# A second matmul layer as seven block products for eight, on pairs of token tiles, in a kernel of twelve expert passes

## The chip, the cores and the metric

The kernel runs as one program on one core of a Trainium2 chip. The metric is the device time of one execution in microseconds, the median of several; smaller is better.

## The reference, cut to what matters

Everything is float32. There are two samples of 2048 tokens with 512 channels. Two shared experts and one expert chosen per sample are each a two-layer network with a hidden width of 2048; a softmax gate per sample mixes their three outputs, and a second layer, with a 512 x 512 matrix chosen per sample, follows. Both layers have a residual.

```
dense(x, wi, wo) = relu(x @ wi) @ wo
s0, s1 = dense(x, swi[0], swo[0]), dense(x, swi[1], swo[1])
eo     = dense(x, wi[label[b]], wo[label[b]])
w      = softmax(relu(concat(eo[:, 0], s0[:, 0], s1[:, 0]) @ g1) @ g2)
x      = x + eo * w[0] + s0 * w[1] + s1 * w[2]      # the mix
out    = x + x @ W[cat[b]] + bias[cat[b]]            # the second layer
```

## The kernel before, in words

**Blocks and units.** The 4096 tokens are four blocks of 1024. The work is a list of twelve units (n = 0 to 11): the two shared experts on the four blocks (n = 0 to 7), then the chosen experts, two blocks of sample 0 (n = 8, 9) and two of sample 1 (n = 10, 11). A unit is `up` (L762, the first matrix) and `down` (L903, the second). Both already use a seven-product scheme in two levels, so each is 49 products; the sums around them are on VectorE and GpSimd.

**Slots.** The order of all engines is written out by hand. `up` goes through 7 x 14 = 98 slots, each with two matmuls of 128x256; `down` goes through 49 slots (`SLOTS_DN`, L433), each with four. Within every slot, after its matmuls, `step(other_bg)` (L658) takes one step of the *first* generator in the list `other_bg`, up to its next `yield`; only when that one has ended does the next in the list begin. So side work gets one step per slot, 147 steps per unit, in the order in which it was appended.

**Side work at the end.** After unit 8 the gate of sample 0 (`gate`, L1096) and the second layer of its first block (`layer1`, L1185) are appended; after unit 9 the second layer of the next block; at the start of unit 10 the part of sample 1's gate that belongs to the shared experts (`gate_shared`, L1070); after unit 10 sample 1's `gate` and `layer1` of the third block; at the first slot of `down` in unit 11 `premix` (L1228) for the fourth block. At the last slot but one of `down` in unit 11, `prepare` (L1321) empties the list: `while other_bg: step(other_bg)` (L1333). Then `last_layer1` (L1270) does the second layer of the fourth block with nothing beside it.

**`layer1`.** `layer1_weights` (L1144) loads the 1 MB matrix into the buffer tagged "s" (there is one), waits 14 slots, adds the identity to its diagonal (the residual), and makes the bias by a matmul. Then for each of eight tiles of 128 tokens: `fetch` loads four parts of 256 KB (the input and three expert outputs) into one of three buffers, tagged "raw", "o" and "t"; `mix` scales three of them on ScalarE (L1205) and adds them on GpSimd (L1210); `layer1_mm` (L1170) runs four matmuls of 128x512 into one PSUM tile; `layer1_put` (L1178) adds the bias on VectorE and stores. `mix` of a tile is issued a whole tile ahead of its matmuls. One tile takes 7 slots.

**`premix`** loads two 1 MB accumulators, three 1 MB pieces of earlier outputs into the buffers "raw", "o" and "t", then the matrix of the fourth block into "s"; it makes 16 multiply-adds on VectorE (L1251), and a fourth piece is loaded after the first four of them.

All loads and stores named here are issued by SyncE's queue (SP), in order; an instruction there that waits holds up those behind it.

Of the kernel before, what the change touches and what calls it, by code (L numbers as in the profile page):

```python
# [8 lines left out]
F32 = mybir.dt.float32  # L9
AF = mybir.ActivationFunctionType  # L10
# [5 lines left out]
P = 128  # L16
TB = 1024
TQ = 256
NP = 7
ADD, SUB = ALU.add, ALU.subtract  # L20
# [16 lines left out]
def cond_resid_kernel(  # L37
# [22 lines left out]
    nc = tc.nc  # L60
    B, S, D = x.shape
    E, _, F = wi.shape
    NCAT = W.shape[0]
    NX = g2.shape[1]
    DC = D // P
    NG = F // P // 4
    NBB = S // TB
# [10 lines left out]
    bigp = ctx.enter_context(tc.tile_pool(name="big", bufs=1))  # L78
    iop = ctx.enter_context(tc.tile_pool(name="io", bufs=2))
    small = ctx.enter_context(tc.tile_pool(name="small", bufs=1))  # L80
    ps = ctx.enter_context(tc.tile_pool(name="ps", bufs=2, space=PSUM))
# [4 lines left out]
    def read_ids():  # L86
# [22 lines left out]
    units = [(e, blk) for e in range(2) for blk in range(NB)]  # L109
# [12 lines left out]
    xr = {blk: dram.tile([P, 16, TQ], F32, name=f"xr_{blk}") for blk in range(NB)}  # L122

    xs = {blk: dram.tile([P, NP, NP, TQ], F32, name=f"xs_{blk}") for blk in range(NB)}
    ys = {
        (j, blk): dram.tile([P, DC, TB], F32, name=f"ys_{j}_{blk}")
        for j in range(NX)
        for blk in range(NB)
    }
# [526 lines left out]
    prep_bg, other_bg = [], []  # L656
# [400 lines left out]
    gates, hids = {}, {}  # L1057
# [5 lines left out]
    def when(there):  # L1063
        while not there[0]:
            yield

    def when_quiet():
        yield from when(quiet)
# [73 lines left out]
    NT = TB // P  # L1142

    def layer1_weights(blk, lag, also=None):  # L1144

        b = blk // NBB
        brow = small.tile([1, D], F32, tag="brow", name=f"brow_{blk}")
        nc.sync.dma_start(out=brow, in_=bvec[bass.ds(cat[b], 1), :])
        w1 = bigp.tile([P, DC, D], F32, tag="s", bufs=1, name=f"w1_{blk}")
        nc.sync.dma_start(out=w1, in_=W_v[:, bass.ds(cat[b] * DC, DC), :])  # L1150
        bias = small.tile([P, D], F32, tag="bias", name=f"bias_{blk}")
        for k in range(lag):
            yield
            if k == 5 and also:
                also()
        for c in range(DC):
            yield from when_quiet()
            v = w1[:, c, c * P : (c + 1) * P]
            nc.vector.tensor_tensor(v, v, ident, ADD)
            if c % 2:  # L1160
                yield
        pb = ps.tile([P, D], F32, tag="m", name=f"pb_{blk}")
        nc.tensor.matmul(pb, lhsT=ones[0:1, :], rhs=brow, start=True, stop=True)
        nc.vector.tensor_copy(bias, pb)
        l1[blk] = (w1, bias)
        yield

    l1, po = {}, {}

    def layer1_mm(blk, t, mixed):  # L1170
        po[t] = ps.tile([P, D], F32, tag="m", name=f"po_{blk}_{t}")
        for c in range(DC):
            nc.tensor.matmul(  # L1173
                po[t], lhsT=mixed[c], rhs=l1[blk][0][:, c, :],
                start=(c == 0), stop=(c == DC - 1),
            )

    def layer1_put(blk, t):  # L1178
        b, t0 = divmod(blk, NBB)
        o = iop.tile([P, D], F32, tag="xn", name=f"o_{blk}_{t}")  # L1180
        nc.vector.tensor_tensor(o, po[t], l1[blk][1], ADD)
        r0 = t0 * TB + t * P
        nc.sync.dma_start(out=out[b, r0 : r0 + P, :], in_=o)

    def layer1(blk, lag):  # L1185
        b = blk // NBB
        mixed = {}
        xv = xr[blk].rearrange("p (c q) t -> p c q t", c=DC)

        def fetch(t):  # L1190
            m = bigp.tile(
                [P, 4, DC, P], F32, tag=("raw", "o", "t")[t % 3], bufs=1, name=f"mix_{blk}_{t}"
            )
            q, h = divmod(t, 2)
            nc.sync.dma_start(out=m[:, 3, :, :], in_=xv[:, :, q, h * P : (h + 1) * P])
            for j in range(NX):
                nc.sync.dma_start(
                    out=m[:, j, :, :], in_=ys[j, blk][:, :, t * P : (t + 1) * P]
                )
            mixed[t] = m  # L1200

        def mix(t):
            m = mixed[t]
            for j in range(NX):
                nc.scalar.activation(  # L1205
                    m[:, j, :, :], m[:, j, :, :], AF.Copy, scale=gates[b][:, j : j + 1]
                )
            yield
            for j in range(NX):
                nc.gpsimd.tensor_tensor(m[:, 3, :, :], m[:, 3, :, :], m[:, j, :, :], ADD)  # L1210
                yield

        yield from layer1_weights(blk, lag, lambda: (fetch(0), fetch(1)))
        yield from mix(0)
        for t in range(NT):
            if t + 2 < NT:
                fetch(t + 2)
            if t + 1 < NT:
                yield from mix(t + 1)
            layer1_mm(blk, t, [mixed[t][:, 3, c, :] for c in range(DC)])  # L1220
            yield
            yield
            layer1_put(blk, t)
            yield

    acc = {}

# [63 lines left out]
    with tc.manual_schedule():  # L1291


        zero = small.tile([1, 512], F32, tag="brow", name="zero")
        nc.vector.memset(zero, 0.0)
        for k in range(2):
            pz = ps.tile([P, 512], F32, tag="z", name=f"prime_{k}")
            nc.tensor.matmul(pz, lhsT=ones[0:1, :], rhs=zero, start=True, stop=True)
        y = yp.tile([P, DC, 4, TQ], F32, tag="y", name="y_0")
        x_rest = first_x()  # L1300
        next(x_rest)
        begin = First(y)
        read_ids()
        xg = x_sums(0)
        advance(xg)
        fetch_w(7)
        begin.outer((5,))
        other_bg.append(("x0", x_rest))
        for n, (e, blk) in enumerate(units):
            if n == 0:  # L1310
                for e0, k0 in [(e0, k0) for e0 in range(1, NE) for k0 in range(2)]:
                    preps[e0, k0] = Prep(e0, k0)
            tops = {}
            if n in (2 * NB, 2 * NB + NBB):
                other_bg.append((f"s{n}", gate_shared((n - 2 * NB) // NBB, 13 if n == 2 * NB else 6)))
            if n:
                y = yp.tile([P, DC, 4, TQ], F32, tag="y", name=f"y_{n}")
            H = up(n, xg, tops, y)
            coming = {}

            def prepare(s, n=n, y=y):  # L1321
                m = n + 1
                if n == 0 and s == 30:

                    preps[1, 0].begin()
                elif n == 0 and s == len(SLOTS_DN) - 1:
                    begin.flush()
                    prep_bg.extend(preps.values())
                if m == len(units):
                    if s == 0:  # L1330
                        other_bg.append(("pre", premix(units[n][1], 10)))
                    elif s == len(SLOTS_DN) - 2:
                        while other_bg:  # L1333
                            step(other_bg)
                        for t in LAST[:2]:
                            last_mix(units[n][1], y, t)
                    return
                if m in MAKES:
                    if s == 0:
                        coming["x"] = load_x(m, 2)  # L1340
                    if s % 2 == 0:
                        next(coming.get("x", iter(())), None)
                    if s == 44:
                        for _ in coming.get("x", ()):
                            pass
                        coming["s"] = x_sums(m)
                    if s >= 44 and "r" not in coming and advance(coming["s"], 1):
                        coming["r"] = True
                elif s in (30, 38):
                    fetch_parts(m, I_UP(m)[(s - 30) // 8])  # L1350

            down(n, H, tops, y, prepare)
            if n + 1 < len(units):
                xg = coming.get("s")
                if xg and "r" not in coming:
                    advance(xg)
            if e >= 2:
                b = e - 2
                while prep_bg:
                    for part in "ost":  # L1360
                        prep_bg[0].force(part)
                    prep_bg.pop(0)
                if blk % NBB == 0:
                    other_bg.append((f"g{b}", gate(b, 8)))
                if n + 1 < len(units):
                    other_bg.append((f"l{blk}", layer1(blk, 14)))
        while other_bg:
            step(other_bg)
        last_layer1(blk, y)
# [30 lines left out]
```

## Time and profile before

| | us |
|---|---|
| median of 3 runs (2220.66 to 2226.8) | 2224.69 |
| the profiled execution | 2226.44 |
| its span | 2224.7 |
| TensorE matmuls busy | 2187.0 (98%) |
| VectorE busy | 1620.0 (73%) |
| GpSimd busy | 812.9 (37%) |
| ScalarE busy | 545.1 (25%) |

The granted TensorE clock is 0.997 of full. On the page, a busy share of an engine is its own time, and a group's line gives the busy sum, the mean of one, and the idle time of the engine ahead of the group with what ended it. The chain of waits is the one that ended last, followed back. A float32 matmul stands in the trace as two weight-load and matmul pairs, so four matmuls are "x8"; the time between starts, and not the duration of one, is its cost, since they overlap.

### The profile page before, as it was taken

To read this page: it belongs to the slowest core of one execution; us is meant where nothing else is said; L and a number is where in the kernel's file an instruction comes from. 1 tells how busy PE (TensorE), PEld (TensorE's weight loads), DVE (VectorE), ACT (ScalarE), POOL (GpSimd) and SP (SyncE) were. 2 spreads that over 40 slices of the span, in tenths; PEclk is the share of its full clock that TensorE was granted. 3 is DMA by queue.
4 is the path that set the end of the run, shared out by engine and by line. 5 is a ranking of instruction groups with operands and counts; after the bars stand their busy time and mean duration, and the time that the engine had idled before them with its cause. 6 is when DMAs were issued, how large, how long until landed. Compare 5 with 4: busy or idle time off the path is not lost.

```text
span 2224.7 us, 29251 instructions
## 1 busy us (share of the span) xinstructions
PE 2187.0 (98%) x9808; PEld 1853.9 (83%) x9808; DVE 1620.0 (73%) x2047; ACT 545.1 (25%) x937; POOL 812.9 (37%) x1259
## 2 busy tenths in 40 slices
PE   8999999999999999999999999999999999999999
PEld 6887888888888888888888888888877877887785
DVE  7897787688587587588577588588676746867695
ACT  3221231331321321231231141131133133213310
POOL 6777443852840540450450451360033023002400
PEclk9999999999999999999999999999999999999999
DMA  9853996997996996896997997897896697679681
GB/s 343 302 189 96 333 336 214 340 332 231 298 305 214 317 315 200 281 329 189 292 313 221 303 314 225 272 330 218 297 296 193 185 314 238 179 240 312 219 281 52
DMA packets 484256, 581.59 MB, mean 261 GB/s; under 512 B 28552, under 2 KB 316296, under 8 KB 480908
## 3 DMA queue, kind: packets, MB, share of 16 engines
q1 hardware_dynamic: 480380, 572.91, 79.5%
q10 hardware_dynamic: 3728, 6.82, 0.9%
q8 instruction: 80, 1.31, 0.2%
q14 instruction: 68, 0.56, 0.1%
HBM read 421.80 MB, written 157.81 MB: 261 GB/s over the span
## 4 chain that ended last, share of the span: by engine, by line
PE 84%; DVE 8%; DMA 3%; POOL 1%; issue 1%; SPq 1%; ACT 0%; DVEq 0%; POOLq 0%
PE ux L819 23%; PE dx L954 23%; PE dy L954 11%; PE uy L819 11%; PE dz L954 6%; PE uz L819 6%; PE po L1173 5%; DVE h L925 1%; DVE h L795 1%; SPq L186 1%; DVE t L757 1%; DMA w<-ws_t 1%; DMA w<-in_L_cond_W_dram 1%; DVE t L752 1%; DMA xn<-in_x_dram 1%
## 5 line engine op out<-in xcount | busy, mean ns | idle before, releaser
L819 PE MATMUL ux<-xs,w 128*128 128x256 f32 x1792 | 426.3, 380 | 10.9 <-DMA w<-ws_t 2.7
L954 PE MATMUL dx<-t,w 128*128 128x256 f32 x1680 | 397.4, 379 | 3.3 <-DVE ds L976 3.2
L819 PEld LDWEIGHTS ux<-xs,w 128*128 128x128 f32 x1792 | 338.8, 190 | 71.2 <-issue 10.3
L954 PEld LDWEIGHTS dx<-t,w 128*128 128x128 f32 x1680 | 318.1, 190 | 48.7 <-issue 2.4
L1210 POOL TENSOR_TENSOR mix<-mix 128x512 f32<-128x512 f32 x72 | 110.1, 1531 | 443.0 <-DMA mix<-ys 246.5
L842 DVE TENSOR_TENSOR us<-ux,h 128x512 f32<-128x512 f32 x240 | 163.4, 687 | 129.2 <-PE ux L819 128.9
L925 DVE TENSOR_TENSOR h<-h,h 128x1024 f32<-128x1024 f32 x192 | 245.6, 1294 | 0.0
L789 ACT ACTIVATE h<-h 128x1024 f32<-128x1024 f32 x156 | 164.0, 1055 | 232.5 <-DVE h L847 122.8
L819 PE MATMUL uy<-xs,w 128*128 128x256 f32 x896 | 212.2, 379 | 0.6 <-DVE h L866 0.6
L847 DVE TENSOR_TENSOR h<-uy,us 128x512 f32<-128x512 f32 x168 | 116.0, 691 | 122.5 <-ACT us L840 118.3
L700 POOL TENSOR_TENSOR seen<-pulse 1x1 f32<-1x1 f32 x33 | 16.5, 499 | 512.4 <-DVE pulse L699 469.1
L819 PEld LDWEIGHTS uy<-xs,w 128*128 128x128 f32 x896 | 170.1, 190 | 27.3 <-issue 1.8
L853 ACT ACTIVATE h<-uz 128x512 f32<-128x512 f32 x168 | 99.5, 592 | 356.1 <-PE uz L819 318.3
L954 PE MATMUL dy<-h,w 128*128 128x256 f32 x672 | 160.3, 382 | 4.2 <-DVE y L978 4.1
L819 PE MATMUL ux<-xi,w 128*128 128x256 f32 x640 | 155.4, 386 | 6.8 <-POOL idle L149 2.3
L954 PEld LDWEIGHTS dy<-h,w 128*128 128x128 f32 x672 | 127.7, 191 | 23.0 <-issue 5.2
L954 PE MATMUL dx<-h,w 128*128 128x256 f32 x616 | 145.5, 379 | 0.0
L954 PE MATMUL dz<-h,w 128*128 128x256 f32 x616 | 145.5, 379 | 0.0
L819 PEld LDWEIGHTS ux<-xi,w 128*128 128x128 f32 x640 | 121.8, 192 | 27.7 <-issue 4.1
L866 DVE TENSOR_TENSOR h<-uy,us 128x512 f32<-128x512 f32 x168 | 112.2, 686 | 44.3 <-PE uy L819 42.4
L141 POOL TENSOR_TENSOR po<-pr 128x384 f32<-128x384 f32 x48 | 54.8, 1141 | 229.8 <-DMA w<-ws_s 63.0
L954 PE MATMUL dy<-t,w 128*128 128x256 f32 x576 | 136.1, 379 | 0.0
(155 smaller groups left out, 3425.2 us busy)
## 6 DMA issues: line engine op xcount, KB each, us to landing
w<-ws_t SPq DMA_DIRECT2D x352, 256.0 KB, 4.2
w<-ws_s SPq DMA_DIRECT2D x270, 256.0 KB, 4.0
w<-ws_o SPq DMA_DIRECT2D x264, 256.0 KB, 5.2
xs<-xs SPq DMA_DIRECT2D x56, 896.0 KB, 7.4
ws_s<-ps SPq DMA_DIRECT2D x24, 1024.0 KB, 8.5
ws_t<-pt SPq DMA_DIRECT2D x24, 1024.0 KB, 9.5
ys<-y SPq DMA_DIRECT2D x11, 2048.0 KB, 7.8
ws_o<-po SPq DMA_DIRECT2D x24, 768.0 KB, 6.6
```

Source lines behind the costliest of these rows:

```text
L141: eng.tensor_tensor(o, i0, i1, op)
L186: nc.sync.dma_start(out=raw[:, q, b, :, :], in_=src[:, k, :, :])
L789: nc.scalar.activation(v, v, AF.Relu)
L819: nc.tensor.matmul(p[:, g, :], lhsT=wt[:, 2 * d + g, :], rhs=x_ops[n, i, k], start=first and g == 0, stop=True, skip_group_check=True,)
L842: nc.vector.tensor_tensor(t, p, half(src, 12 if k == 6 else 22, d), ADD)
L847: nc.vector.tensor_tensor(half(dst, 22, d), bank["y", d], t, ADD)
L853: nc.scalar.activation(half(dst, 11, d), p, AF.Relu if i in final else AF.Copy)
L866: nc.vector.tensor_tensor(half(dst, 12, d), p, sn["b", d], ADD)
L925: nc.vector.tensor_tensor(bl(o), bl(i0), bl(i1), SUB)
L954: nc.tensor.matmul(p, lhsT=wt[:, g, :], rhs=op[g], start=first and g == 0, stop=True, skip_group_check=True,)
L1173: nc.tensor.matmul(po[t], lhsT=mixed[c], rhs=l1[blk][0][:, c, :], start=(c == 0), stop=(c == DC - 1),)
L1210: nc.gpsimd.tensor_tensor(m[:, 3, :, :], m[:, 3, :, :], m[:, j, :, :], ADD)
```

## The change

The second layer of blocks 0 and 1 (run beside units 9 and 10) goes through the new `layer1_fast`; the third block keeps `layer1`, and the fourth `last_layer1`.

- **Matmuls.** Two token tiles and the matrix are split into 2 x 2 quarters. A pair of tiles takes seven products, each two matmuls of 128x256, in place of eight matmuls of 128x512.
- **Sums.** Per block four VectorE sums of the matrix quarters (`layer1_sums`); per pair four GpSimd sums of the tiles, two more for `u2b`, and seven VectorE sums of 128x256 in place of two of 128x512.
- **Buffers.** The three buffers have four places each; three hold the parts of a tile and the fourth one sum of the matrix. So the third expert output is loaded into the place of the first (`part(t, 2)`) after that has been added.
- **Order.** A pair is: `mix` of its second tile (9 steps), `layer1_pair` (11 steps) with the `mix` of the next pair's first tile between them, two `fetch`, 4 empty steps.

```diff
+    def layer1_sums(blk, spaces):
...
+        for o, x0, x1 in ((t3, b22, b12), (b12, b12, b11), (t2, b22, b12), (t4, b21, t2)):
+            yield from when_quiet()
+            nc.vector.tensor_tensor(o, x0, x1, SUB)
+            yield
...
+    def layer1_pair(blk, m0, m1, t):
...
+        for o, x0, x1, op in (
+            (s1, a21, a22, ADD), (s2, s1, a11, SUB), (s3, a11, a21, SUB), (s4, a12, s2, SUB),
+        ):
+            nc.gpsimd.tensor_tensor(o, x0, x1, op)
+            if o is s2:
+                yield
+        yield
+        lhs = {1: a11, 2: a12, 3: s4, 4: a22, 5: s1, 6: s2, 7: s3}
...
+        mm(pa[:, 0], 1, True)
+        mm(pa[:, 1], 6)
+        yield
+        yield
+        nc.vector.tensor_tensor(p1, pa[:, 0], bias[:, TQ:], ADD)
+        nc.vector.tensor_tensor(u2, pa[:, 1], p1, ADD)
+        nc.gpsimd.tensor_tensor(u2b, u2, bias[:, :TQ], ADD)
+        nc.gpsimd.tensor_tensor(u2b, u2b, bias[:, TQ:], SUB)
...
+        mm(pb[:, 0], 5, True)
+        mm(pb[:, 1], 7)
+        yield
+        yield
...
+        nc.vector.tensor_tensor(u4, pb[:, 0], u2, ADD)
+        nc.vector.tensor_tensor(o1[:, 1], pb[:, 1], u4, ADD)
+        yield
+        mm(pa[:, 0], 2)
+        mm(pb[:, 0], 3)
+        mm(pb[:, 1], 4)
+        yield
+        yield
...
+    def layer1_fast(blk, lag):
...
+        def mix(t):
+            scale(t, 0)
+            scale(t, 1)
+            yield
+            add(t, 0)
+            yield
+            add(t, 1)
+            yield
+            part(t, 2)
+            for _ in range(4):
+                yield
+            scale(t, 2)
+            yield
+            add(t, 2)
+            yield
...
+        fetch(2)
+        for t in range(0, NT, 2):
+            yield from mix(t + 1)
+            ahead = mix(t + 2) if t + 2 < NT else iter(())
+            for _ in layer1_pair(blk, m[t], m[t + 1], t):
+                next(ahead, None)
+                yield
+            for k in (t + 3, t + 4):
+                if k < NT:
+                    fetch(k)
+            if t + 2 < NT:
+                left = 0
+                for _ in ahead:
+                    left += 1
+                    yield
+                for _ in range(4 - left):
+                    yield
...
-                    other_bg.append((f"l{blk}", layer1(blk, 14)))
+                    layer = layer1_fast if n + 2 < len(units) else layer1
+                    other_bg.append((f"l{blk}", layer(blk, 14)))
```

## The prediction, made before the changed kernel was run

> **What bounds the kernel now.** I read the page's busy line, then the chain of waits, then the groups by line.
>
> ```profile
> PE 2187.0 (98%) x9808; PEld 1853.9 (83%) x9808; DVE 1620.0 (73%) x2047; ACT 545.1 (25%) x937; POOL 812.9 (37%) x1259
> ...
> PE 84%; DVE 8%; DMA 3%; POOL 1%; issue 1%; SPq 1%; ACT 0%; DVEq 0%; POOLq 0%
> ```
>
> TensorE is busy for 98% of the span, so a matmul less is time less, and any new wait of TensorE is time more. The chain in order of time shows the second layer inside unit 9:
>
> ```profile
> 1641.02 3.43 PE po L1173 x8
> 1644.45 1.73 PE ux L819 x8
> 1646.18 1.73 PE uy L819 x8
> 1647.90 1.73 PE ux L819 x8
> 1649.63 0.86 PE uz L819 x4
> 1650.49 3.43 PE po L1173 x8
> ```
>
> A tile's four matmuls of 128x512 cost 3.43 us; four of 128x256 cost 1.73; 7 slots of two (0.864 us each) lie between tiles, and nothing waits. The end of the chain shows what stands hidden behind `down` of unit 11 today, and what does not:
>
> ```profile
> 2106.64 3.43 PE po L1173 x8
> ...
> 2121.95 14.03 DMA w<-in_L_cond_W_dram
> 2135.98 0.02 issue
> 2136.00 0.49 DVE w L1159 x2
> ...
> 2141.24 0.66 DVE acc L1251
> ...
> 2191.58 1.73 PE dy L954 x8
> 2193.30 27.48 PE po L1173 x64
> ```
>
> The third block's last tile is done at 2110; `premix` starts its loads at 2117.03, its matrix lands at 2135.98, its 16 multiply-adds (0.66 us apart where nothing lies between) run beside matmuls until 2170; then the last 64 pairs run alone. All of `premix` is free because it starts 75 us ahead of its need.
>
> **The change part by part.**
>
> *Matmuls.* Old: 8 tiles x 3.43 = 27.4 us per block. New: 4 pairs x 14 matmuls x 0.432 = 24.2. Saved 3.2 per block, **-6.5 us** in all. The Trainium skill, "TensorE: Matmul & The Clock Gate", section "Back-to-back issue gap", speaks against this: in a stream of weight load and matmul it gives about 81 ns for 128 columns and 131 for 512, so half the columns cost more than half the time; an estimate from it (about 98 ns at 256) would make 112 short pairs 31% dearer than 64 long ones, +17 us for the two blocks in place of -6.5. The rows have 216 ns beside 429, and I go by them.
>
> *VectorE, SyncE, ScalarE.* Per pair seven sums at 0.42 (the L978 row's shape) for two at 0.68: +1.6 us, over 24 slots for 14; plus four 0.68 us sums per block. VectorE is busy 47.5 of 70 us in the stage at 1640, and now the second layer is spread thinner: nothing, at most 0.5 us per pair where a product waits for u4. Loads, scalings and adds keep their numbers.
>
> *The slots.* This is the part that decides. A step of side work costs a slot. Old, per block: weights 17, first mix 4, seven tiles of 7, one of 3: 73 steps. New: 17 + 9 + three pairs of 24 + a last one of 20 = 118. A unit has 147. Unit 9: gate 25 + 118 = 143, it just fits. Unit 10: 118, and `gate_shared` needs 64 more: about 35 spill into `up` of unit 11, where it moves only in the slots marked spare (three of 14) once per 7. The order of instructions of the built kernels agrees (positions, no times): the gate's matmul in unit 11 stands after slot 15 of `up` before and after slot 88 now. 57 slots are left; the rest of the gate takes some 10, the third block 73, and `premix` 29. So in the built order the tiles 3 to 7 of the third block and the whole of `premix` stand behind the last slot but one of `down`, emptied there at a stroke:
>
> ```
> before                               after
> po_6 (third block)                   dx_4 x4  (last slot but one)
> 3 slots of down                      po_3, po_4, po_5, po_6, po_7
> po_7                                 pb  (bias of the fourth block)
> 46 slots of down                     dy_4 x4  (last slot)
> po_4 (fourth block) ...              po_4 (fourth block) ...
> ```
>
> *The price of that.* Let T0 be the end of the last slot but one (2191.6 before). It comes earlier by the five tiles (17.2), the bias matmul (1.05) and the saving (6.5): 2166.85. After it, with nothing beside:
> - Tiles 3 to 5 are loaded in time: TensorE to T0+10.3. The load for tile 6 stands on SP behind the store of tile 3, which waits for VectorE at T0+4.3. Four issues 2.3 us, landing 3.3 (the lowest of the L1197 row, as traffic is low), ScalarE and adds of 1.27 on GpSimd (the lowest and median of L1210): tile 6 starts near T0+13.1, tile 7 at T0+17, ends T0+20.4; VectorE and the store's issue: T0+21.7.
> - Only then does SP reach the loads of `premix`. Before, 18.95 us passed from the first one (2117.03) to the landing of the matrix, at some 385 GB/s and with other tiles between; 6.3 MB at 385 GB/s are 16.4, with a start 18: T0+39.7.
> - Diagonal and bias 1.6; 16 multiply-adds x 0.66 = 10.6, and the fourth piece, asked for after the first four, may be a little late (0 to 2.2); `last_mix` 0.87. The last products start at **T0+54** (50 to 60: 16 us for the loads at the slice's 424 GB/s at the lower end; the highest landing of L1197, 7.8, and a late fourth piece at the upper).
> - From there to the end of the span 31.4, as before.
> Sum: 2166.85 + 54 + 31.4 = 2252.2, **+27.5 us** with the saving in it.
>
> *The new wait inside a pair.* Product 6 needs the second GpSimd sum of the second tile, whose third part is loaded only after the first was added. GpSimd's shape, from the row of the early sums of x, is 0.73 (median):
>
> ```profile
> L384 POOL TENSOR_TENSOR xi<-x x40: 717/728/1708, 10.2 to 631.3; 128x256 f32<-128x256 f32 x40
> ```
>
> The adds of the mix (first fence, L1210) and the landing of its loads (second, L1197), lowest, median and highest:
>
> ```profile
> L1210 POOL TENSOR_TENSOR mix<-mix x72: 1260/1274/2271, 1635.1 to 2102.1; 128x512 f32<-128x512 f32 x72
> ```
>
> ```profile
> L1197 SPq DMA_DIRECT2D mix<-ys x72: 518/651/2948, 1624.1 to 2090.0; - x72
> ...
> DMA to landing us min/median/max: 3.3/5.2/7.8
> ```
>
> From the load's issue to product 6 are 8 slots and one product, 7.8 us; landing 5.2 + scale 0.72 + add 1.4 + two sums 1.46 = 8.8: a stall of 1. Where the tile's first parts were fetched only 4 slots ahead of its mix (pairs 2 and later), the chain from the fetch is 1.1 + 5.2 + 0.72 + 1.35 + 5.2 + 0.72 + 1.4 + 1.46 = 17.2 against 15 slots and a product, 13.8: a stall of 3.4. In `down` a slot is twice as long and none is left. By the built order five pairs lie in `up`: the first of each block, and three later ones. 2 x 1 + 3 x 3.4 = **+12 us**. Bounds: 0 with all landings at 3.3, 20 with GpSimd at its means (1.53 and 0.95) and the 0.5 of VectorE. Behind the waiting adds on GpSimd stand only this layer's own; on ScalarE, which waits for the part's landing, stand copies that empty PSUM for TensorE (next section); on SP, which waits for the add, weight tiles with 12 buffers, some 20 us ahead. The skill, "DMA: Bandwidth & Descriptors", section "Anatomy of one DMA — SWDGE (gpsimd) path", has 2.0 us + bytes/436e9 (for another issue path): an estimate of 2.6 us for 256 KB, by which the stall would vanish and the sum be 2252. The row has twice that, and I go by the row.
>
> **Sum.** -6.5 is in the 27.5; 27.5 + 12 = +39.5 on the profiled execution's span of 2224.7 (2226.44 with what lies around it, 1.75 above the median). On the median of 2224.69: **2264 us**.
>
> **The rivals.**
> - *The saving stands alone*: if the emptied list were hidden, -6.5: 2218, faster. It decides if `premix` is loaded before T0. The order of SP speaks against it: its loads stand behind the store of tile 7. 3%.
> - *Tail yes, pair stalls no*: parts land at 3.3 to 4: 2252. It decides if no landing in `up` is above some 3.5. Within the range; 18%.
> - *ScalarE as the bound*: its waits of about 2.8 us at a late fetch and some 4 at the third part hold back the copies that empty PSUM, and TensorE waits for each: five pairs x 6.8 = 34 for 12: 2286. For it: ScalarE already waits 29.7 us for these loads. Against: TensorE's own waits on ScalarE from 1620 on add up to 0.6 us today, and the part of `up` where ScalarE empties most (its first and fifth seventh) holds one pair only. 12%.
> - *The change does not bind* (side work is elastic): 2225. The slot count speaks against it. 2%.
>
> **How the numbers follow.** The forecast with its bounds: low 27.5 - 4 + 0 = 23.5, high 27.5 + 6 + 20 = 53.5, so 2248 to 2278. The forecast has 65%, which with the second rival's 18% makes some 80% in that range; the third lies above, the first and fourth below. A measurement here tells 0.3%, 6.7 us, from no change: faster 3%, same 2%, slower 95%.
>
> **What would show it.** Right: between the last slots of `down` and the last 64 pairs some 34 us of TensorE idle (54 less the five tiles, the bias and the last slot), ended by VectorE's multiply-adds, and ahead of those the landing of the fourth block's matrix; pairs of products at 0.432 us a matmul; idle of TensorE before product 6, ended by GpSimd. Wrong: TensorE over 98% busy to the end, or the idle time in units 9 and 10 above 25 us, ended by ScalarE.

## The result, and the profile after

The changed kernel takes 2286.0 us (median of six runs, 2285.3 to 2293.2) for 2224.2 before (2220.2 to 2226.8): 1.029 times as long, 95% interval 1.0279 to 1.0304. The prediction was slower, 2264, with 2278 as its upper end; the time lies 8 us above that.

The page's busy line and shares of the chain, after:

```profile
PE 2194.7 (96%) x9904; PEld 1875.5 (82%) x9904; DVE 1653.6 (72%) x2095; ACT 546.6 (24%) x937; POOL 863.8 (38%) x1307
...
PE 80%; DVE 8%; DMA 5%; POOL 3%; SPq 2%; issue 1%; ACT 0%; POOLq 0%; DVEq 0%; ACTq 0%
```

TensorE's share has gone from 98 to 96%. There are fewer columns to multiply, yet its busy sum has risen by 7.7 us; that is the first hint that some matmuls ran slower. What it waited for (engine, tile, line, then releaser: us in total, times, longest):

```profile
PE pb L1163 <- DMA brow<-in_L_cond_b_dram: 17.4, 1, 17.4
PE po L1249 <- DVE acc L1407: 9.5, 1, 9.5
...
PE pa L1206 <- POOL mix_raw L1197: 5.7, 1, 5.7
PE pa L1206 <- POOL mix_t L1197: 5.5, 2, 3.1
...
PE pa L1206 <- POOL mix_o L1197: 4.8, 1, 4.8
PE pb L1206 <- DVE o L1228: 3.8, 5, 1.1
PE po L1249 <- POOL mix L1286: 3.6, 1, 3.6
```

The first, second and last lines are the tail behind the last slots; the four in `pa` and `pb` are waits inside the pairs: product 6 for the GpSimd sum s2 (16.0 us in four waits), and product 3 for VectorE's u4 and the sum made from it in the next line (L1228, which ends the wait; 3.8 in five). The end of the chain:

```profile
2209.56 8.77 PE po L1249 x16
...
2226.61 11.59 DMA w<-in_L_cond_W_dram
...
2250.99 29.13 PE po L1249 x64
```

Tiles 6 and 7 of the third block, then the matrix of the fourth, then the last 64 pairs, all with nothing beside them, where before they lay beside `down`.

The part ahead of unit 9 is the same code in all kernels, and its end varied between 1582 and 1593 us from profile to profile. So I use **the stage**: from the first slot of unit 9 (timeline) to the start of the last 64 pairs (chain). It is 604.2 us before (1589.1 to 2193.3) and 668.6 after (1582.4 to 2251.0): +64.4. What TensorE does not spend on its own matmuls at their usual pitch I call idle; up to the last slots of `down` in unit 11 it is 8.5 us before and 43.9 after.

### The profile page after: what moved, and what is told of

It is laid out like the page before. It is cut to its first block, busy times and chain, and to the rows that moved or that the text cites. A ratio compares the mean times of both kernels' runs of the same rounds, so it can differ in the third digit from the quotient of the medians.

```text
span 2283.9 us, 29576 instructions
## 1 busy us (share of the span) xinstructions
PE 2194.7 (96%) x9904; PEld 1875.5 (82%) x9904; DVE 1653.6 (72%) x2095; ACT 546.6 (24%) x937; POOL 863.8 (38%) x1307
## 4 chain that ended last, share of the span: by engine, by line
PE 80%; DVE 8%; DMA 5%; POOL 3%; SPq 2%; issue 1%; ACT 0%; POOLq 0%; DVEq 0%; ACTq 0%
PE dx L954 23%; PE ux L819 20%; PE dy L954 12%; PE uy L819 9%; PE dz L954 6%; PE uz L819 5%; PE po L1249 2%; DVE h L795 1%; DVE h L925 1%; PE pb L1206 1%; DMA mix_raw<-ys 1%; SPq L186 1%; POOL xi L384 1%; PE pa L1206 1%; DVE h L866 1%
## 5 line engine op out<-in xcount | busy, mean ns | idle before, releaser
L925 DVE TENSOR_TENSOR h<-h,h 128x1024 f32<-128x1024 f32 x192 | 252.2, 1329 | 0.0
L795 DVE TENSOR_TENSOR h<-h,h 128x1024 f32<-128x1024 f32 x96 | 130.0, 1354 | 3.7 <-ACT h L853 2.4
```

Source lines behind the costliest of these rows:

```text
L795: nc.vector.tensor_tensor(o, blk_of(O[22], cc), blk_of(O[21], cc), ADD)
L925: nc.vector.tensor_tensor(bl(o), bl(i0), bl(i1), SUB)
```

## The experiments

| kernel | median, us | ratio, 95% interval | stage, us | against 604.2 |
|---|---|---|---|---|
| after | 2286.0 | 1.0279 to 1.0304 | 668.6 | +64.4 |
| first_only | 2231.1 | 1.0027 to 1.0055 | 615.2 | +11.0 |
| second_only | 2281.7 | 1.0252 to 1.0286 | 657.0 | +52.8 |
| steps_only | 2261.8 | 1.0153 to 1.0187 | 639.7 | +35.5 |
| no_overflow | 2255.6 | 1.0133 to 1.0167 | 640.0 | +35.8 |
| apart | 2239.0 | 1.0062 to 1.0094 | 618.1 | +13.9 |
| no_third_load | 2245.0 | 1.0079 to 1.0128 | 627.1 | +22.9 |
| vector_only | 2241.2 | 1.0047 to 1.0099 | 621.2 | +17.0 |
| bare_products | 2227.8 | 1.0009 to 1.0031 | 609.4 | +5.2 |
| vector_more | 2229.1 | 1.0009 to 1.0040 | 607.0 | +2.8 |
| made_waits | 2251.4 | 1.0123 to 1.0161 | 634.5 | +30.3 |
| made_waits_filled | 2252.0 | 1.0109 to 1.0151 | 633.6 | +29.4 |
| waits_filled | 2255.2 | 1.0118 to 1.0161 | 637.2 | +33.0 |

Line numbers in an experiment's profile are those of its own kernel. Each stage is read from one profiled execution, while the median is of four to ten runs, so differences of a few us between two stages are to be held against the medians.

### Tail and pairs apart: four kernels

`first_only` and `second_only` give the new layer to one block each:

```diff
-                    layer = layer1_fast if n + 2 < len(units) else layer1
+                    layer = layer1_fast if n == 8 else layer1      # first_only
+                    layer = layer1_fast if n == 9 else layer1      # second_only
```

> The new layer for the first block alone (beside unit 9), the old one for the second and third. Steps: unit 9 takes 25 + 118 = 143 of 147, unit 10 takes 73 + 64 = 137, unit 11 takes 25 + 73 + 29 = 127, so nothing spills. My theory (the spill costs about 37 us behind the last slots, the waits inside the pairs about 31 in both blocks, the products save 6.5): no idle time before the last 64 pairs, 3.2 us saved, and the idle time that the changed kernel showed in unit 9 stays (11.8 + 2.2 us, for 1.4 + 0 before): 2224 - 3.2 + 12.6 = 2233 us, between 2228 and 2237. Rival A (the price is in the seven products themselves, or in their sums, and the slots matter little): half of the whole loss, 2224 + 31 = 2255. Rival B (the pairs' waits are an accident of the second block): 2221.

> The new layer for the second block alone (beside unit 10). Steps: unit 10 needs 118 + 64 = 182 of 147, 35 spill; unit 11 needs 35 + 25 + 73 + 29 = 162, so the spill behind the last slots is the one of the changed kernel. My theory: the tail costs the same 37 us, the pairs of unit 10 cost 20 to 22, the products save 3.2: 2224 + 37 + 21 - 3 = 2279 us, between 2272 and 2284; with the first block's kernel of the same series the two losses add up to that of both (62). Rival A (price in the products): 2255, the same as the first block alone. Rival B (waits only where both blocks have it): 2258.

`steps_only` is the kernel before with empty steps (its `layer1` line stays):

```diff
+                    if n + 2 < len(units):
+                        other_bg.append((f"e{blk}", iter([None] * 45)))
```

> The kernel before, with its products and buffers unchanged, and 45 empty steps behind the second layer of the first and of the second block (73 + 45 = 118 steps, as many as the new layer takes). The instructions are those of the kernel before; only their order against the slots moves. My theory: the tail comes alone, tiles 3 to 7 of the third block and the whole of the fourth block's mix stand behind the last slots: 2224 + 34, or + 37 with the slower clock seen there, 2258 to 2262 us (range 2254 to 2266), and no waits inside units 9 and 10. Rival A (slots of side work are elastic, the loss comes with the products): 2224. Rival B (the tail is more than I think, since the waits in units 9 and 10 were partly hidden): above 2270.

`no_overflow` is the changed kernel with this in `down`:

```diff
             step(other_bg)
+            if n == 10 and s >= 20:
+                step(other_bg)
```

> The changed kernel, with a second step of side work in each of the last 29 slots of the second matrix of unit 10. By then the second block's layer has ended, so that only steps of the gate for the shared experts are doubled: unit 10 has 176 steps for 182, some 6 spill, and unit 11 needs 133 of 147. My theory: the tail goes and the pairs' waits stay: 2286 - 37 = 2249 us, between 2244 and 2254; in the profile no idle time of over 3 us between the last slots and the last 64 pairs, and the same 30 to 36 us of it in units 9 and 10. Rival A (the tail is the whole loss): 2218. Rival B (the tail is not set by the spill): 2280 and over.

Measured: 2231, 2282, 2262 and 2256 for 2233, 2279, 2260 and 2249 expected; the price in the products alone, the elastic steps and the tail as the whole loss all fall. `steps_only` has no instruction of the new layer, and its chain ends in the same way:

```profile
2203.40 11.60 DMA w<-in_L_cond_W_dram
...
2216.52 7.95 DVE acc L1251 x12
...
2227.73 29.90 PE po L1173 x64
```

The matrix's landing and VectorE's multiply-adds hold the last products, and these take 29.90 us for 27.48. So the tail costs 35.5 us in the stage and 2.4 behind it. In `no_overflow` it is gone: a slot of `down` runs up to the last products.

```profile
2220.86 1.73 PE dy L954 x8
2222.59 27.59 PE po L1251 x64
```

The stages add up. The first block's pairs cost 11.0 + 3.2 (the saving) = 14.2, the second's 52.8 - 35.5 + 3.2 = 20.5, together **34.7 us for the 12 predicted**; 34.7 + 35.5 - 6.5 = 63.7, against 64.4 measured. The medians give the pairs the same sum (2231.1 less 2222.7 of its series, and 2281.7 less the 2261.8 of `steps_only`, each with 3.2 added: 11.6 + 23.1). So do the two profiles alone: after, units 9 and 10 take 427.7 us for 400.0, with 6.5 us less of products (34.2 for the pairs), and unit 11 takes 240.9 for 204.2 up to the last 64 pairs, with as many matmuls (36.7 for the tail). `no_overflow` has 35.8 + 6.5 = 42.3 of idle beyond before's, 7.6 more than the pairs' 34.7: units 9 and 10 take 430.4 us, 2.7 more than after, as product 6 waits 18.8 us for 16.0, and its unit 11, where the third block and `premix` now stand at other slots, takes 209.6 for 204.2.

### What the pairs wait for

`no_third_load` is `no_overflow` with that load taken away and the rest left:

```diff
-            part(t, 2)
```

> The kernel without the spill (second step of side work at the end of unit 10), with the load of the third part left out: its place is scaled and added as it stands, so that the mix of the first two blocks holds the first output twice in place of the third. All matmuls, sums, scalings and steps stay. My theory: it is the landing of that load which product 6 waits for. Without it the five or six waits on GpSimd of 1 to 5.6 us go (19 us), and the slow stretches after them (some 9 us); the waits on u4 (3 us) and uz (2) stay: 2255 - 28 = 2227 us, between 2222 and 2233. Rival A (GpSimd itself is late, with six sums a pair more): 2250 and over. Rival B (the half-speed matmuls are of the pairs and not of the waits): 2236.

`apart` keeps the work and puts more slots between the load and its use; so that nothing spills, `gate_shared` of sample 1 goes to a list of its own (`beside`), stepped once per slot of `down` in unit 10, with its loads in other buffers (not shown):

```diff
+    FAR = {(0, 2): 6, (1, 0): 6, (1, 2): 6, (1, 4): 6}
...
-            for _ in range(4):
+            for _ in range(4 + far):
                 yield
...
         nc.vector.tensor_tensor(o1[:, 1], pb[:, 1], u4, ADD)
         yield
+        if (blk, t) in FAR:
+            yield
```

> The changed layer for both blocks, with more slots where its pairs stand in the first matrix of units 9 and 10 (pair 1 of the first block, pairs 0, 1 and 2 of the second): six more steps between the load of the third part and its scaling, and one more between the sum u4 and product 3. So that nothing spills, the gate for the shared experts takes a step of its own in each slot of the second matrix of unit 10, beside the second layer, with buffers of the weight ring for its loads. My theory (product 6 waits for GpSimd because the third part lands late, the wait is at most 5.7 us, and the slow matmuls come after waits): six slots are 5.2 us, so the waits of product 6 fall from 19 us in all to under 2, the waits on u4 go, and with them the slow stretches; what is left of the 36 us of idle time in these units is about 3 (one wait of 2.2 for VectorE's uz). 2224 - 6.5 + 3 = 2220 us, between 2215 and 2227. Rival A (the waits are set by the number of steps on SP, ScalarE or GpSimd and not by the distance): 2245 to 2256. Rival B (waits gone, but the matmuls of 128x256 in the pairs are slower anyway): 2230.

Both fell short: 2245 for 2227, and 2239 for 2220. Without the load the waits of product 6 fall from 18.8 to 6.3 us and the stage by 12.9, but waits on VectorE stay about as they were. Nor do the slow matmuls go that are shown below: 8.2 us with the load, 8.4 without, since the waits that are left are followed by them too. Waits in the stage with the load (`no_overflow`), then of the whole execution without it:

```profile
PE pa L1208 <- POOL mix_t L1199: 7.0, 2, 3.7
PE pa L1208 <- POOL mix_raw L1199: 6.5, 2, 5.6
PE pa L1208 <- POOL mix_o L1199: 5.3, 1, 5.3
```

```profile
PE pb L1208 <- DVE o L1230: 3.8, 5, 1.1
PE pa L1208 <- POOL mix_o L1199: 3.5, 1, 3.5
...
PE pa L1208 <- POOL mix_raw L1199: 2.4, 1, 2.4
```

So the late third part is a cause, and a third of the loss, not all of it. In `apart` product 6 still waits 7.2 us, and TensorE's waits on VectorE add up to 10.9 in the stage. For the longest of these waits (3.18 us, second pair of the second block) the queues show why. SyncE issued the third part at 1871.62; ScalarE scaled it only at 1880.78, and stood like this just ahead (start, duration, and in brackets the idle time and what ended it):

```profile
1877.28 1.06 ACT L791 ACTIVATE h<-h 128x1024 f32<-128x1024 f32 x1 [2.96 <-DVE h L849]
1878.24 0.58 ACT L855 ACTIVATE h<-uz 128x512 f32<-128x512 f32 x1
1878.72 2.15 ACT L791 ACTIVATE h<-h 128x1024 f32<-128x1024 f32 x2
1880.78 0.71 ACT L1335 ACTIVATE mix_raw<-mix_raw,g 128x512 f32<-128x512 f32 x1
```

Six slots later in ScalarE's queue the scaling came behind four activations of the unit's own, one of them itself waiting 2.96 us for VectorE. The distance was bought in slots, and part of it was lost in an ordered queue. My expectation had counted only the landing.

Next the sums are cut off, without the third load and on top of one another, GpSimd's first (`vector_only`; the two for `u2b` go too):

```diff
-            nc.gpsimd.tensor_tensor(o, x0, x1, op)
...
-        lhs = {1: a11, 2: a12, 3: s4, 4: a22, 5: s1, 6: s2, 7: s3}
+        lhs = {1: a11, 2: a12, 3: a12, 4: a22, 5: a21, 6: a21, 7: a11}
```

> The kernel without the third load, and now also without the GpSimd sums of the pairs (the four sums of tile quarters, of which the products take plain quarters instead, and the two for u2b, for which u2 stands): the output of the first two blocks is not the reference's. All products, all VectorE sums and all steps stay. I measure from the first slot of unit 9 to the start of the last products (604.2 us before, 627.1 without the third load), since the part ahead varies from run to run by some 5 us. Theory now (what is left after product 6 has its operands is VectorE: with about 9 us more work per block it is late for sums that the units' own matmuls wait for): the 6.3 us of waits on GpSimd and about 3 of slow stretches go, the waits on VectorE stay: 617 us, between 613 and 621; 2234 us in all. Rival A (VectorE's added sums cost nothing): 600, 2220 in all. Rival B (it is the steps or the products themselves): as the bare products, whatever they give.

then VectorE's (`bare_products`):

```diff
-            nc.vector.tensor_tensor(o, x0, x1, SUB)
...
-        nc.vector.tensor_tensor(p1, pa[:, 0], bias[:, TQ:], ADD)
-        nc.vector.tensor_tensor(u2, pa[:, 1], p1, ADD)
...
-        nc.vector.tensor_tensor(u4, pb[:, 0], u2, ADD)
```

> The same with VectorE's sums cut too: four sums per pair (one for each quarter of the output) for seven, no sums of the matrix quarters, no u4 that product 3 has to wait for. Left are the seven products of each pair at their places, the scalings and adds of the mix and the stores; the output of the first two blocks is not the reference's. Theory: nothing waits any more, and the stage from unit 9 to the last products is the one before less the saving: 604.2 - 6.5 = 598 us, between 596 and 604; 2218 us in all (2215 to 2224). Rival (matmuls of 128x256, as short products between others, are dearer than half of 128x512, or the step doubled at the end of unit 10 has a price of its own): 608 and more, 2230 in all.

and the kernel before gets a like amount of VectorE work (`vector_more`, in `layer1_put`):

```diff
+        for _ in range(3 if blk < 2 else 0):
+            nc.vector.tensor_tensor(o[:, :TQ], po[t][:, :TQ], l1[blk][1][:, :TQ], ADD)
```

> The kernel before, with three more VectorE sums of 128x256 per tile in the first two blocks (each writes a part of the output tile again, with the same values): 8 x 3 x 0.42 = 10 us of VectorE work more per block, about what the seven products bring (11.8 + 2.7 - 5.4 = 9.1). Products, loads, GpSimd and steps are those of before. Theory (VectorE's added work alone makes TensorE wait, since VectorE is already busy for 47.5 of 70 us here and works in order): the stage from unit 9 to the last products becomes 610 to 616 us for 604.2, 2230 to 2236 in all. Rival (VectorE has room for it, its waits in the pairs come only from standing behind late products): 604 to 607, 2224 to 2227 in all.

In the stage: 640.0 with everything, 627.1 without the third load (-12.9), 621.2 without GpSimd's sums (-5.9), 609.4 without VectorE's (-11.8). The medians go 2255.6, 2245.0, 2241.2, 2227.8; the runs of the second and the third overlap (2238.8 to 2251.5 and 2234.7 to 2248.0), so the step of GpSimd's sums is not clear of the scatter, and the other two are. TensorE's waits on VectorE within the stage, `vector_only` first, `bare_products` second:

```profile
PE pb L1207 <- DVE o L1227: 2.7, 4, 1.0
PE ux L819 <- DVE uz L836: 2.7, 3, 1.7
...
PE ux L819 <- DVE us L842: 1.9, 2, 1.6
PE uy L819 <- DVE h L866: 1.8, 1, 1.8
```

```profile
PE ux L819 <- DVE uz L836: 1.7, 2, 1.1
...
PE ux L819 <- DVE us L842: 1.4, 2, 1.2
```

The wait on u4 goes, and the waits for the unit's own sums (uz, us, h) fall from 6.4 to 3.1. The slow matmuls after waits fall as well, from 5.0 us to 1.7. But `vector_more` fell near its rival, with 607.0 at its upper end: a like amount of VectorE work costs only 2.8 us in the stage where no product stands behind it. The median of 2229.1 lies between the two theories, 5.6 above the 2223.5 of its series. So VectorE's price in the pairs is for the greater part not its work but its place. The sums on which the next product waits are part of it (2.7 us, shown). That the sums which wait in VectorE's order for a late product hold up the unit's own sums behind them fits the rest, and is only argued.

`bare_products` missed 598 too. Of its 11.7 us of idle beyond before's, two waits for the adds of the mix itself (2.3 and 0.8) and the slow matmuls after the first make some 5; the rest are waits on VectorE and ScalarE, most of them in unit 11, which takes 208.8 us for 204.2 here, as it does in `no_overflow`. But units 9 and 10 alone take 400.6 for 400.0 too, where the saving by itself would make 393.5. The bare products, with no sums of tiles, matrix or products beyond the bias, are 0.2% slower than before (1.0009 to 1.0031). This order of steps could not have gained even with free sums, and no experiment points to a version that beats the kernel before.

### Matmuls at half speed after a wait

The first pair of the second block, in the changed kernel's timeline of TensorE (a group of x4 is two matmuls, 0.86 us from start to start):

```profile
1828.41 1.03 PE L1206 MATMUL pa<-w,mix_raw 128*128 128x256 f32 x4
1835.13 2.07 PE L1206 MATMUL pa<-mix_raw 128*128 128x256 f32 x4 [5.69 <-POOL mix_raw L1197]
1836.99 1.91 PE L819 MATMUL uy<-xs,w 128*128 128x256 f32 x4
1838.70 1.91 PE L819 MATMUL ux<-xs,w 128*128 128x256 f32 x4
1840.41 1.23 PE L1206 MATMUL pb<-w,mix_raw 128*128 128x256 f32 x4
```

Product 6 waits 5.69 us, and then three groups take 1.86, 1.71 and 1.71 us each: 2.7 us lost in them after the wait has ended. The granted clock in this stretch (the column after the five engines' busy times) is half:

```profile
1835.00:1840.40 5.40, 5.27 (x12) 4.21 (x13) 1.42 (x3) 0.73 (x1) 3.92 (x5) 0.50 0.23 63
```

In units 9 and 10 five such stretches cost some 9.6 us; in the tail the clock is 0.72, and the last 64 pairs take 29.13 us for 27.48. To see if the wait does it, and not the pairs, waits were made in the kernel before (`made_waits`; `made_waits_filled` has FILL = [0, 1, 0, 2, 0, 4, 0, 6]), in `layer1_mm`:

```diff
+    WAITS = [0, 3, 0, 6, 0, 9, 0, 15]
+    FILL = [0] * 8
...
+        if blk == 0 and WAITS[t]:
+            first = lambda v: nc.tensor.matmul(
+                po[t], lhsT=v, rhs=l1[blk][0][:, 0, :], start=True, stop=True
+            )
+            first(mixed[0])
+            for k in range(WAITS[t]):
+                nc.gpsimd.tensor_tensor(mixed[0], mixed[0], ones, ALU.mult)
+            for k in range(FILL[t]):
+                first(ident)
```

> The kernel before, with waits made by hand in the second layer of the first block: ahead of tiles 1, 3, 5 and 7 one more matmul of 128x512 into the tile's own output (overwritten by the real ones), and after it 3, 6, 9 and 15 multiplications by one of the tile's first chunk on GpSimd (128x128, an estimate of 0.4 us each, half of the 0.73 us of a 128x256), for which the tile's matmuls wait. Waits of about 1.5, 2.7, 3.9 and 6.3 us, 14 in all, and 3.4 us for the four matmuls. Theory (the granted clock falls by a wait of over some 2 to 3.5 us and the matmuls after it run at half speed for some 3 us): the stretches after the two long waits lose another 1.5 to 3 us each, the third some 1, none after the shortest: 2224 + 18 + 7 = 2249 us. Rival (the half speed belongs to the pairs of products): no slow matmuls here, 2242.

> The same waits made by hand, with 1, 2, 4 and 6 further matmuls of 128x512 (0.86 us each, overwritten by the real ones) put into them, so that TensorE is busy for most of each wait. The time until the tile's matmuls may start is the same. Theory (idle time of TensorE makes the clock fall): no slow matmuls behind the waits: 2224 + 18 = 2242 us, 7 below the kernel with empty waits. Rival (slow for another reason, such as traffic or GpSimd's port): no difference between the two.

The four tiles with an empty wait (a tile's eight records take 3.60 to 3.70 us at full speed):

```profile
1646.08 3.70 PE L1185 MATMUL po<-w,mix 128*128 128x512 f32 x8 [2.04 <-POOL mix L1181]
...
1671.76 5.28 PE L1185 MATMUL po<-w,mix 128*128 128x512 f32 x8 [5.59 <-POOL mix L1181]
...
1698.25 5.68 PE L1185 MATMUL po<-w,mix 128*128 128x512 f32 x8 [4.84 <-POOL mix L1181]
...
1727.48 6.42 PE L1185 MATMUL po<-w,mix 128*128 128x512 f32 x8 [8.03 <-POOL mix L1181]
```

No pairs and no new sums here, and the tiles after the three long waits are slow by 1.6 to 2.8 us, the one after 2.04 us is not. In `made_waits_filled`, with the same work on GpSimd, three waits are left at 0.80, 1.42 and 2.91 us, and the tiles after them take 3.70 us. Traffic is no rival: from 1727 to 1733 us in `made_waits` the DMA share is 0.00 and the clock 0.50. The theory of the clock holds. As a comparison of times the two kernels tell nothing (2251 and 2252): the filling was too short for one wait, 3.91 us, after which 3.1 us were lost again, and matmuls of no use take time themselves. A last try on the pairs:

```diff
+    FILL = {(0, 2): 7, (1, 0): 12, (1, 2): 8, (1, 4): 12}
...
+        for _ in range(FILL.get((blk, t), 0)):
+            nc.tensor.matmul(
+                pa[:, 0], lhsT=ident, rhs=rhs[1][:, 0, :],
+                start=True, stop=True, skip_group_check=True,
+            )
         mm(pa[:, 0], 1, True)
```

> The kernel without the spill (stage from unit 9 to the last products 640.0 us, 2255.5 in all), with matmuls of no use put ahead of product 1 of the four pairs whose product 6 waited longest (3.3, 5.6, 3.7 and 5.3 us): 7, 12, 8 and 12 of 128x256 (0.432 us each), written to product 1's place and overwritten by it. The operands of product 6 come when they came; TensorE is busy for most of the time until then. Theory (a wait of more than some 3.5 us lets the granted clock fall, and the 128x256 matmuls after it run at half speed): the three slow stretches of 2.7, 2.9 and 1.9 us go, the stage falls by 7.5 to 632 us and the time to 2248, though TensorE does 17 us more work. Rival (half speed belongs to the pairs, or to the data traffic at these places): no gain, 640 or more in the stage, 2255 or more.

The slow stretches after product 6 fell from 8.2 us (three) to 1.8 (one), and the two `up` phases together by some 5 us (109.5 + 129.9 to 108.3 + 126.0). In the stage 2.8 of that are left, since another slow stretch of 1.8 us came in unit 9 after a wait of 1.87 us for VectorE, and none in the whole time (2255 for 2256; 2248 was expected). The share of the clock is shown in the stages; as a remedy it is worth nothing here.

## Why the prediction was wrong, point by point

- **The matmuls, -6.5: right by its rows.** Where the clock is full, a product of two matmuls takes 0.86 us from start to start, also between the unit's own. By the estimate from the Trainium skill ("TensorE: Matmul & The Clock Gate", section "Back-to-back issue gap") the short products alone would have been 17 us dearer. That did not appear: the bare products bring the stage to 5.2 us above before's, waits included.
- **The slots and the tail: right.** From T0 (the end of the last slot but one) to the last products 54 us were predicted and 55.5 measured, from there to the end 31.4 and 32.9. By itself the tail was worked out as 27.5 + 6.5 = 34 and costs 35.5 (`steps_only`), and 2.4 more by the slower last products, which I had not seen coming.
- **"VectorE ... nothing, at most 0.5 us per pair where a product waits for u4": wrong.** The waits that end with the sum after u4 are 0.4 to 1.1 us each, four of the five over 0.5, and all of VectorE's sums in the pairs are worth 11.8 us in the stage.
- **The pair stalls, 2 x 1 + 3 x 3.4 = 12: this is the term that failed.** Product 6 for itself waited 16.0 us, a third over in sum, and not pair by pair: the first pair of the first block had none for 1, the first of the second 5.7 for 1. But the term is 34.7, since the step counted one wait only. Left out were TensorE's waits on VectorE, which the prediction put at nothing or 0.5 us a pair (3.8 us at u4 and 4.1 for the unit's own sums, 1.0 of such before), and the slow matmuls after the waits (9.6 us): in the profile of units 9 and 10, 16.0 + 3.8 + 4.1 + 9.6 = 33.5. The upper bound of 20 was made of the same one wait at its worst, so the range missed as well.
- **The rival of ScalarE** gave 2286, which is the measured number by luck, and is wrong all the same: TensorE's waits on ScalarE add up to 0.8 us after. What it describes can happen, though: in `second_only` ScalarE stood 4.89 us until a part had landed, and TensorE waited 4.18 us for the activation behind that scaling, once. Otherwise ScalarE matters one step earlier, as a queue in which the scaling of a part stands behind others (`apart`). My sign for being wrong, over 25 us of idle in units 9 and 10, did come, but ended by GpSimd and VectorE.
- **Sum.** -6.5 + 35.5 + 34.7 = 63.7 in the stage (64.4 measured) and 1.7 for the last products; the profiled execution came to unit 9 some 6.7 us earlier than that of before, which makes its difference 59.2, and the medians differ by 61.8.

Open: of the 11.8 us of VectorE's sums, 2.7 are waits at u4, 3.3 waits for the unit's own sums and 3.3 slow matmuls; where the rest lies, and which sum held up which, was not followed.

## What to carry to other kernels

Where side work is dealt out one step per slot, count the steps before the multiplications: 45 more steps per block, empty ones, cost 39 us here, six times what seven products for eight can save. A chain of load, scaling, adds and sums between two products of a full TensorE is to be priced in every queue it passes, and a stall of a few us by its length and by the slow matmuls after it. Before building such a scheme, time its bare products at their places: if these do not gain, the scheme in that order will not either.

## What the runs showed of the hardware that was not expected

After a wait of TensorE the granted clock can fall to 0.50, and two matmuls of 128x256 then take 1.71 us for 0.86. The ten waits of 3.7 to 8.0 us that I followed were all succeeded by it, at 1.6 to 3.1 us each; of the waits between 1.8 and 3.5 us some were (1.87, 1.88, 2.42, 3.07) and some were not (2.04, 2.18, 2.91, 3.18, 3.33).

The granted clock as the traces record it shows what decides. Within one execution its changes lie whole multiples of 3.41 us apart, as if time were cut into fixed stretches of 3.41 us, and where these lie differs from one execution to the next. What counts is how much of one stretch TensorE is idle, and not how long a wait is. In the fourteen profiles, without the first 30 us, all 58 stretches at full clock with over 2.0 us of idle were followed by half clock, 6 of the 31 with 1.7 to 2.0 us, and 2 of some 8950 with less (both with about 1.0 us and a matmul of one row of 1.1 us). So the wait of 1.87 us in `waits_filled`, which lies within one stretch, was followed by half clock (columns as in the window above: the first after the length is TensorE's busy time, the clock stands third from the end):

```profile
1773.40:1776.81 3.41, 1.54 (x8) 1.04 (x7) 3.27 (x4) 0.38 (x1) 3.17 (x3) 1.00 0.77 267
1776.81:1780.22 3.41, 3.41 (x10) 2.70 (x9) 0.41 (x1) 0.00 (x0) 0.00 (x0) 0.50 0.02 5
```

The wait of 3.33 us in `no_overflow` was not, since it is cut into 1.96 and 1.37 us:

```profile
1676.65:1680.06 3.41, 1.45 (x7) 0.95 (x5) 2.43 (x4) 2.43 (x5) 1.48 (x2) 1.00 0.87 247
1680.06:1683.48 3.42, 2.05 (x10) 1.82 (x10) 0.00 (x0) 0.97 (x3) 3.34 (x5) 1.00 0.00 1
1683.48:1686.89 3.41, 3.41 (x17) 3.02 (x16) 1.45 (x3) 0.58 (x1) 2.69 (x4) 1.00 0.50 154
```

The Trainium skill, "TensorE: Matmul & The Clock Gate", section "Part 1: The HAM clock gate (the "warmup" mystery)", describes a gate that halves the clock after an idle window of about 3.4 us, free-running, and opens it after as long a busy one. The half, the length and the lack of a fixed point agree with these runs; that a window need not be idle throughout, and 2.0 of its 3.41 us are enough, does not follow from that rule.
